# Mamba's x projection on the two column halves of the TensorE array, each with half of the tokens

## The chip, the cores and the metric

The kernel runs on one core of one Trainium2 chip. Its time is the device time of one launch in microseconds, taken as the median of three runs. The five engines of the core are named as in the profile: PE (TensorE, with its weight loads as PEld), DVE (VectorE), ACT (ScalarE), POOL (GpSimd) and SP (SyncE, which here issues the DMAs). Each works through its own instructions in order and waits on semaphores for the others.

## The reference

The program is a network of two blocks on an input of 4 images, 128 channels and 64 x 64 positions. Block 0 is a deformable neighbourhood attention followed by a recurrence over the 4096 positions; block 1 is a stack of eight Mamba layers followed by a mixture of experts. The change lies in the Mamba layers alone:

```python
def _mamba_layer(x, Wi, cw, cb, Wx, Wdt, bdt, Alog, Dp, Wo):
    xz = x @ Wi
    xi, z = jnp.split(xz, 2, axis=-1)                  # 256 channels each
    ...
    xc = jax.nn.silu(xc)                               # causal convolution of 4 taps before it
    dbl = xc @ Wx                                      # 256 -> 8 + 16 + 16
    dt_r = dbl[..., :DT_RANK]
    Bs = dbl[..., DT_RANK:DT_RANK + D_STATE]
    Cs = dbl[..., DT_RANK + D_STATE:]
    dt = jax.nn.softplus(dt_r @ Wdt + bdt)             # 8 -> 256
    dA = jnp.exp(dt[..., None] * A)
    dBx = (dt * xc)[..., None] * Bs[:, :, None, :]
    _, h = jax.lax.associative_scan(comb, (dA, dBx), axis=1)
    y = jnp.einsum('blds,bls->bld', h, Cs) + Dp * xc
    y = y * jax.nn.silu(z)
    return y @ Wo
```

"The x projection" is `xc @ Wx`: 256 channels in, 40 numbers out for each token.

## The kernel before

**Bodies.** The Mamba part works in bodies. A body is one layer of one image for 512 consecutive tokens (`TL`), and there are 8 chunks x 8 layers x 4 images = 256 of them. Channels lie on the 128 partitions, in two halves `h` (`NH` = 2). Everything is float32; a float32 matmul stands in the trace as two records of one call, a transpose as one.

**Slots.** A body has 16 slots `j`, one for each pair of states of one channel half. Per slot, PE makes the inputs of a scan (`inputs`, L1042, 8 calls with 64 rows each, or for one pair of states ACT writes the decay there instead), ACT makes the decays (`exps`, L1020), DVE runs two scans (`scan`, L1075), POOL multiplies by C every second slot (`times_c`, L1100), and PE adds the products up by transposing them into one bank (`add_up`, L1104). The inputs for slot j + 1 are issued in slot j, into one of two PSUM buffers; the adding up lags four slots behind.

**The rest of a body** (projections, convolution, gate, output projection, norm) is laid into the slots by a list written by hand, `PLAN`, one row a slot. `o` is the body that scans, `n` the next one, `q` the one before. Each row has a part ahead of the adding up and a part behind it. The rows that matter here are those of slots 7 to 13:

```
q.po1 n.edges o.by1 q.square q.pm | n.pz0 q.rstd
n.pz1 n.silu_z0 n.silu n.silu_z1 n.pd0 n.pd1 n.keep s.rr |
n.bt q.ru s.first n.spread n.B n.skip0 |
| q.u n.diag q.end
n.pt0 n.softplus0 n.pt1 n.dtx0 | o.leave0 n.softplus1
o.back0 o.x3 | z.fetch
| n.C0
```

(The first is slot 7; the fifth is slot 11, and slot 12 follows.) So `pd` (the x projection, `xproj`, L933) and `keep` (L939) belong to slot 8, B's transposes `bt` (`turn_b`, L994) and `spread` (L1003, L1009) to slot 9, the step's projection `pt` (`step_proj`, L967) and `softplus` (L973) to slot 11. In the profile a piece of a slot stands behind the scan inputs that are issued in the same slot.

**The recurrence of block 0** runs inside the same bodies: one of its steps is a small matmul (L683) and a tanh on ACT (L691), some 16 a body. Its last step is at 12,811 us; about 34 bodies follow without it.

**The layout before.** The projection's weights stand in the columns 0 to 39 of a 128-column block, with the 8 columns for dt a second time in the columns 64 to 71. `xproj` makes two calls, one per channel half, over all 512 tokens. `keep` copies all 128 rows of the result to SBUF (`dbl`, 512 columns), reordered in blocks of 64 tokens, and sends B and C to memory (`c_d`). `turn_b` transposes four blocks of 128 columns. `spread` takes 14 of the B columns and sends them by two DMAs onto the diagonals of a matrix in memory (`spare`), from which `diag` (L1014) fetches the moving operand of L1042. `step_proj` makes one call per channel half over all tokens, with the rows 0 to 63 for half 0 and 64 to 127 for half 1.

**Banks.** The pieces outside the scans share two PSUM banks, f0 and f1 (`BANK`): `pd` is in f1, `bt` in f0, `pt0` in f1, `pt1` in f0, and `back0` (L1132), the transpose back of the finished half of `o` in slot 12, in f0.

**SP** issues for each body two DMAs to `c_d`, two to `spare`, one `Bb`, one `diag` and four `Cb`, in that order (and others now and then).

Of the kernel before, what the change touches and what calls it, by code (L numbers as in the profile page):

```python
# [8 lines left out]
F32 = mybir.dt.float32  # L9
BF16 = mybir.dt.bfloat16  # L10
AF = mybir.ActivationFunctionType
# [9 lines left out]
P = 128  # L21
# [20 lines left out]
NH = 2  # L42
DI = NH * P
NS = 16
RK = 8
# [658 lines left out]
W_I, W_Z, W_X, W_DT = 0, DI, 2 * DI, 2 * DI + NH * P  # L704
# [42 lines left out]
def mamba(tc, ops, I, rec, x2_d, x3_d):  # L747
# [8 lines left out]
    nc = tc.nc  # L756
    NSLOT = NS // 2 * NH
    NB = TL // P
    HQ = TL // 2
    SP = NS // 2  # L760
    SP_B = SP - 1
    ND = 2 * SP_B
    AHEAD, LAG, HOLD = 3, 4, 2
    with ExitStack() as ctx:
# [4 lines left out]
        w = ctx.enter_context(tc.tile_pool(name="mwk", bufs=2))  # L769
# [3 lines left out]
        w1 = ctx.enter_context(tc.tile_pool(name="mw1", bufs=1))  # L773
# [7 lines left out]
        bdt = c.tile([P, DEPTH, NH], F32, name="bdt")  # L781
# [30 lines left out]
        def bank(what):  # L812

            name = f"f{BANK[what]}"
            return psf.tile([P, TL], F32, tag=name, name=name)
# [6 lines left out]
        def blocks(ap):  # L822

            return ap.rearrange("p (q b t) -> p b q t", q=2, b=NB)
# [103 lines left out]
        def xproj(o, h):  # L928

            if h == 0:  # L930
                o.pd = bank("pd")
            at = W_X + h * P
            nc.tensor.matmul(  # L933
                o.pd, o.given[:, at : at + P], o.xc[:, h, :], start=h == 0, stop=h == NH - 1
            )

        def keep(o):
            o.dbl = w1.tile([P, NB, 2, 64], F32, tag="dbl", name="dbl")
            nc.scalar.copy(o.dbl, blocks(o.pd))  # L939
            o.c_d = dr.tile([2 * NS, TL], F32, tag="c_d", name="c_d")  # L940
            for q in range(2):
                nc.sync.dma_start(
                    out=o.c_d[:, q * HQ : (q + 1) * HQ].rearrange("s (n t) -> s n t", n=NB),
                    in_=o.dbl[RK : RK + 2 * NS, :, q, :],
                )

        def give_b(o):
# [11 lines left out]
            )  # L959

        def step_proj(o, h):
            if h == 0:
                o.pt = {}
            o.pt[h] = bank(f"pt{h}")
            at = W_DT + h * P
            rows = slice(h * 64, (h + 1) * 64)
            nc.tensor.matmul(  # L967
                blocks(o.pt[h]), o.given[rows, at : at + P], o.dbl[rows], start=True, stop=True
            )

        def softplus(o, h):
            o.dt[h] = w3.tile([P, TL], F32, tag="dt", name="dt")
            nc.scalar.activation(o.dt[h], o.pt[h], AF.Softplus, bias=bdt[:, o.l, h : h + 1])  # L973

        def step_x(o, h):
            if h == 0:
# [13 lines left out]

        def turn_b(o):
            o.BT = bank("bt")
            for n in range(NB):
                nc.tensor.transpose(  # L994
                    o.BT[:, n * P : (n + 1) * P],
                    o.dbl[:, n].rearrange("p q t -> p (q t)"),
                    ops.ident,
                )

        def spread(o):  # L1000

            small = w.tile([P, NB, ND], F32, tag="bts", name="bts")
            nc.scalar.copy(small, o.BT.rearrange("p (n r) -> p n r", n=NB)[:, :, RK : RK + ND])  # L1003
            o.spare = spares[bodies.index(o) % len(spares)]
            for q in range(2):
                half = o.spare[q * 64 : (q + 1) * 64]
                line = half.ap[0][0]
                to = bass.AP(half.tensor, half.offset, [[line + ND, 64], [64 * ND, NB], [1, ND]])
                nc.sync.dma_start(out=to, in_=small[q * 64 : (q + 1) * 64])  # L1009

        def diag(o):

# [160 lines left out]
        def get(i):  # L1173
            return bodies[i] if 0 <= i < len(bodies) else None

        def table(name):
            return lambda o: nc.scalar.preload_act_table_set(name)

        halves = {
            "v": proj, "pz": proj_z, "silu_z": silu_z, "skip": skip_x, "pd": xproj, "pt": step_proj,  # L1180
            "softplus": softplus, "dtx": step_x, "turn": turn, "leave": leave, "back": turn_back,
            "gate": times_gate, "po": out_proj,
        }
# [7 lines left out]
            "fetch": fetch, "mean": mean, "var": lambda o: sums(o, o.x2, "var"),  # L1191
            "rv": lambda o: inverse(o, 1e-6), "rr": lambda o: rows(o, "rr"),
            "first": first_u, "silu": silu_x, "keep": keep, "spread": spread, "diag": diag,
            "B": give_b,
            "bt": turn_b, "square": square, "pm": lambda o: sums(o, o.sq, "pm"),
            "rstd": lambda o: inverse(o, 1e-5), "ru": lambda o: rows(o, "ru"), "u": norm,
            "x3": lambda o: fetch_x(o) if o.l == DEPTH - 1 else None,
# [23 lines left out]
        t = PRE  # L1221
        for i in range(-2, len(bodies) + 1):
            o, n, q = get(i), get(i + 1), get(i - 1)
            who = {"o": o, "n": n, "q": q, "m": get(i + 2), "a": o or q}
            s, z = get(i + 3), get(i + 4)
# [384 lines left out]
def attention_masks():  # L1610


    import numpy as np

    def seen(first, count, window, size):
        start = min(max(first - K // 2, 0), size - window)
        q = np.arange(first, first + count)
        k = np.arange(start, start + window)
        lo = np.clip(q - K // 2, 0, size - K)[:, None]
        return (k[None] >= lo) & (k[None] < lo + K)  # L1620

    r = [seen(f, ROWS, KR, H) for f in (0, ROWS, H - ROWS)]
    c = [seen(f, TC, KC, W) for f in (0, TC, W - TC)]
    m = np.stack([np.einsum("ak,bl->abkl", x, y).reshape(P, NKEY) for x in r for y in c], axis=1)
    return np.where(m, np.float32(0), np.float32(-1e30)).astype(np.float32)


def layouts(a):

    import numpy as np  # L1630

    def halves(v):
        return np.moveaxis(v.reshape(DEPTH, NH, P, *v.shape[2:]), 2, 0)

    f = {k: np.asarray(v) for k, v in a.items()}
    o = {}
    o["x"] = f["x"].reshape(B, P, L).transpose(1, 0, 2)
    o["proj"] = np.stack(
        [f[n].T for n in ("L0_conv_Wq", "L0_conv_Wk", "L0_conv_Wv", "L0_conv_Wo", "L0_ffn_W")],
        axis=1,  # L1640
    )
    o["V"] = f["L0_ffn_V"].T
    vec = [f[f"L0_conv_b{n}"] for n in "qkvo"]
    vec += [np.tile(f[f"L0_conv_{n}"], G) for n in ("off_dw_b", "ln_w", "ln_b")]
    vec += [f["L0_conv_rpe_b"], f["L0_ffn_gamma"], f["L0_ffn_beta"], np.tile(f["L1_ffn_gate_b"], 2)]
    o["vec"] = np.stack(vec, axis=1)
    o["dw"] = np.tile(f["L0_conv_off_dw_w"].reshape(HD, K * K), (G, 1))
    o["rpe"] = f["L0_conv_rpe_w"].reshape(P, 9)
    offw = np.zeros((P, 2, P), np.float32)
    for g in range(G):  # L1650
        ch = slice(g * HD, (g + 1) * HD)
        offw[ch, :, ch] = f["L0_conv_off_pw_w"].T[:, :, None]
    o["offw"] = offw
    o["mask"] = attention_masks()
    w_in = f["L1_conv_W_in"]
    o["m_taps"] = halves(f["L1_conv_conv_w"])
    given = np.zeros((DEPTH, P, W_GIVEN), np.float32)
    given[:, :, W_I : W_I + DI] = w_in[:, :, :DI]
    given[:, :, W_Z : W_Z + DI] = w_in[:, :, DI:]
    for h in range(NH):  # L1660
        ch = slice(h * P, (h + 1) * P)
        given[:, :, W_X + h * P : W_X + h * P + RK + 2 * NS] = f["L1_conv_W_xproj"][:, ch]
        given[:, :, W_X + h * P + 64 : W_X + h * P + 64 + RK] = f["L1_conv_W_xproj"][:, ch, :RK]
        given[:, :, W_OUT + h * P : W_OUT + (h + 1) * P] = f["L1_conv_W_out"][:, ch]
        given[:, h * 64 : h * 64 + RK, W_DT + h * P : W_DT + (h + 1) * P] = f["L1_conv_W_dt"][:, :, ch]
    o["m_given"] = given
    o["m_cb"] = halves(f["L1_conv_conv_b"])
    o["m_bdt"] = halves(f["L1_conv_b_dt"])
    o["m_skip"] = halves(f["L1_conv_D_skip"])
    o["m_A"] = halves(f["L1_conv_A_log"])  # L1670
    o["m_rms"] = f["L1_conv_rms_w"].T
    o["gate"] = f["L1_ffn_gate_w"].T

    w1, w2 = f["L1_ffn_weight1"], f["L1_ffn_weight2"]
    t = w1[:, :P].reshape(2, 4, 4, 2, P, HID).transpose(0, 2, 4, 3, 1, 5)
    o["w1"] = t.reshape(8, P, 8 * HID)
    t = w2[:, :HID].reshape(2, 4, 4, 2, NHC, P, P).transpose(0, 2, 5, 3, 1, 4, 6)
    o["w2"] = t.reshape(8, P, 8 * HID)
    o["b1"] = np.repeat(w1[:, P].reshape(2, P // B, HID), B, axis=1)
    o["b2"] = w2[:, HID].T  # L1680
    return {k: np.ascontiguousarray(v) for k, v in o.items()}
# [16 lines left out]
```

## Time and profile before

| | us |
|---|---|
| median of 3 runs | 14,895.22 (14,884.57 to 14,900.8) |
| the profiled execution | 14,892.08 |
| its span, first to last instruction | 14,890.3 |
| busy DVE, POOL, ACT (share of the span) | 12,974.0 (87%), 12,589.8 (85%), 10,980.2 (74%) |
| x projection, L933: 1,024 records of 128x512 | mean 592 ns |
| pt, L967: 1,024 records of 64x512 | mean 589 ns |
| B's transposes, L994: 1,024 records of 128x128 | mean 287 ns |
| keep, L939: 256 copies of 128x512 | mean 586 ns |
| softplus, L973: 512 of 128x512 | mean 690 ns |
| granted TensorE clock over the span | 0.984 |

A record of PE starts before the one ahead of it has ended, so its duration is a latency; what a record costs is the time from its start to the start of the next. Durations of the other engines overlap by about 0.1 us in the same way.

The Mamba part reaches from about 1,924 us to 14,608 us. The first scans of successive bodies stand 48.6 us apart in most bodies while the recurrence runs, and 49.4 us in every fourth, which also turns a new block of the recurrence's input. After the recurrence they stand 48.3 to 51.4 us apart, 49.8 in the mean.

### The profile page before, as it was taken

The page shows a single profiled execution, that of the slowest core. Times are in us where ns is not written, and L with a number is a line of the kernel's source. Part 1 is how long each engine was busy: PE and PEld are TensorE (multiplying, and loading weights), DVE is VectorE, ACT ScalarE, POOL GpSimd, SP SyncE. Part 2 cuts the span into 40 slices and gives each one's busy share as a digit, 9 for nine tenths or more (in the row PEclk, how much of TensorE's full clock was granted, in tenths as well). Part 3 has the DMA queues.
Part 4 walks back from the last instruction along what each step waited for, and adds up shares of the span by engine and source line. Part 5 has one row for each costly group of instructions (what it writes and reads, how often), then busy time and mean ns, then how long its engine had stood idle before and what let it go on. Part 6 is the DMA issues. An engine that isn't in the chain of part 4 may idle for free. (4 is left out here: it accounts for less than half of the span.)

```text
span 14890.3 us, 307789 instructions
## 1 busy us (share of the span) xinstructions
PE 14160.7 (95%) x124378; PEld 10821.2 (73%) x124378; DVE 12974.0 (87%) x16043; ACT 10980.2 (74%) x21400; POOL 12589.8 (85%) x5760
## 2 busy tenths in 40 slices
PE   7999989999999999999999999999999999999996
PEld 3444467777777777777777777777777777777775
DVE  8997079998999899999998999989999999989994
ACT  6887267777777777777777777777777777777773
POOL 5564079999999999999999999999999999999993
PEclk8999999999999999999999999999999999999998
DMA  0000034434443434343444344344434343434344
GB/s 23 26 26 23 29 122 144 144 136 148 142 147 135 152 137 150 132 151 138 149 142 144 137 149 142 138 145 145 146 136 151 138 149 133 154 131 145 133 146 184
DMA packets 600044, 1914.56 MB, mean 129 GB/s; under 512 B 347488, under 2 KB 347872, under 8 KB 434272
## 3 DMA queue, kind: packets, MB, share of 16 engines
q1 hardware_dynamic: 598480, 1894.60, 36.1%
q8 instruction: 984, 16.12, 0.4%
q14 instruction: 436, 3.57, 0.1%
q10 hardware_dynamic: 144, 0.26, 0.0%
HBM read 1823.10 MB, written 71.57 MB: 127 GB/s over the span
## 5 line engine op out<-in xcount | busy, mean ns | idle before, releaser
L1100 POOL TENSOR_TENSOR hs<-hs,Cb 128x2048 f32<-128x2048 f32 x2048 | 9300.9, 4543 | 749.0 <-DVE state L1092 562.3
L1075 DVE TENSOR_TENSOR_SCAN hs<-dA,state,dBx 128x512 f32<-128x512 f32 x7168 | 8808.2, 1267 | 700.2 <-PE dBx L1042 561.3
L1020 ACT ACTIVATE dA<-dt,A 128x512 f32<-128x512 f32 x7168 | 4730.4, 716 | 11.6 <-DVE hs L1075 5.5
L1104 PE MATMUL yT<-ident,hs 128*128 128x128 f32 x32768 | 4376.9, 277 | 30.4 <-POOL hs L1100 30.2
L1042 PE MATMUL dBx<-diag,dtxT 64*128 64x128 f32 x57344 | 4195.3, 283 | 27.1 <-DVE hs L1075 20.1
L1104 PEld LDWEIGHTS yT<-ident,hs 128*128 128x128 f32 x32768 | 3785.4, 147 | 433.6 <-issue 349.2
L1042 PEld LDWEIGHTS dBx<-diag,dtxT 64*128 64x128 f32 x57344 | 3509.4, 187 | 800.7 <-issue 741.3
L683 PEld LDWEIGHTS p<-z,vt 128*128 128x128 f32 x8192 | 1283.9, 189 | 881.8 <-ACT z L691 401.8
L691 ACT ACTIVATE z<-p 128x4 f32<-128x4 f32 x4096 | 702.3, 171 | 1396.6 <-PE p L683 1368.8
L683 PE MATMUL p<-z,vt 128*128 128x4 f32 x8192 | 1453.7, 248 | 107.1 <-ACT z L691 98.4
L1075 DVE TENSOR_TENSOR_SCAN hs<-dAp,state,hs 128x512 f32<-128x512 f32 x1024 | 1273.3, 1273 | 296.7 <-POOL hs L1063 296.7
L1063 POOL TENSOR_TENSOR hs<-Bb,dtx 128x512 f32<-128x512 f32 x1024 | 1284.9, 1280 | 0.0
L904 DVE SCALAR_TENSOR_TENSOR xc<-f,taps,xc 128x511 f32<-128x511 f32 (+2 forms) x1536 | 1115.8, 726 | 53.4 <-ACT z L691 49.3
L1020 ACT ACTIVATE dAp<-dt,A 128x512 f32<-128x512 f32 x1024 | 708.8, 692 | 491.6 <-DVE hs L1075 470.1
L279 DVE SCALAR_TENSOR_TENSOR acc<-qp,dww,acc 128x512 f32<-128x512 f32 x1184 | 892.4, 754 | 25.6
L979 POOL TENSOR_TENSOR dtx<-dt,xc 128x512 f32<-128x512 f32 x512 | 651.6, 1273 | 217.5 <-ACT dt L973 217.5
L293 POOL TENSOR_TENSOR off<-off,to 128x512 f32<-128x512 f32 x288 | 366.4, 1272 | 412.7 <-ACT to L291 400.0
L1020 ACT ACT_TABLE_LOAD x511 | 655.6, 1283 | 9.0
L898 ACT ACTIVATE xc<-f,taps 128x512 f32<-128x512 f32 x512 | 350.7, 685 | 414.7 <-PE f L895 281.1
L919 PE MATMUL f<-u,given 128*128 128x512 f32 x1024 | 600.6, 670 | 3.8 <-DVE xc L904 3.8
L847 PEld LDWEIGHTS f<-avg,sq 128*128 128x128 f32 x2048 | 257.0, 197 | 466.0 <-ACT sq L1148 466.0
L895 PE MATMUL f<-u,given 128*128 128x512 f32 x1024 | 567.0, 636 | 0.8 <-DVE u L868 0.8
(235 smaller groups left out, 15160.8 us busy)
## 6 DMA issues: line engine op xcount, KB each, us to landing
Cb<-c_d SPq DMA_DIRECT2D x1024, 1024.0 KB, 7.2
diag<-spare SPq DMA_DIRECT2D x256, 1792.0 KB, 8.8
Bb<-c_d SPq DMA_DIRECT2D x256, 512.0 KB, 4.8
given<-in_m_given_dram SPq DMA_DIRECT2D x64, 640.0 KB, 8.6
slab<-in_w_dram SPq DMA_DIRECT2D x60, 512.0 KB, 9.9
x<-x_d SPq DMA_DIRECT2D x96, 256.0 KB, 3.0
c_d<-dbl SPq DMA_DIRECT2D x512, 32.0 KB, 1.6
x_d<-x SPq DMA_DIRECT2D x63, 256.0 KB, 3.2
```

Source lines behind the costliest of these rows:

```text
L279: nc.vector.scalar_tensor_tensor(rows(to), x, dww[:, t : t + 1], rows(o.acc), ALU.mult, ALU.add)
L683: nc.tensor.matmul(self.p[:, k, :], self.vt, self.before, start=False, stop=True, skip_group_check=True)
L691: nc.scalar.activation(self.z[:, k, :], self.p[:, k, :], AF.Tanh, scale=0.5)
L904: nc.vector.scalar_tensor_tensor(x, o.v[h][:, : TL - k], taps[:, o.l, h, DC - 1 - k : DC - k], x, ALU.mult, ALU.add)
L919: nc.tensor.matmul(o.pz[h], o.given[:, at : at + P], o.u, start=True, stop=True)
L979: nc.gpsimd.tensor_tensor(to, blocks(o.dt[h]), blocks(o.xc[:, h, :]), ALU.mult)
L1020: nc.scalar.activation(o.dA[j][:, k, :], o.dt[h], AF.Exp, scale=A[:, o.l, h, n : n + 1])
L1042: nc.tensor.matmul(o.dBx[j][:, at : at + 64, :], o.dtxT[h][row, n, :], o.diag[row, n, :, 2 * sp : 2 * sp + 2], start=True, stop=True,)
L1063: nc.gpsimd.tensor_tensor(hs[:, k, :].rearrange("p (q n t) -> p q n t", n=NB, q=2), o.Bb[:, k, :].rearrange("p (q n t) -> p q n t", n=NB, ...
L1075: nc.vector.tensor_tensor_scan(hs[:, k, :], o.dA[j][:, k, :], hs[:, k, :] if sp == SP_B else o.dBx[j][:, :, k], state[:, o.l, o.b, h, s : ...
L1100: nc.gpsimd.tensor_tensor(hs, hs, o.Cb[f], ALU.mult)
L1104: nc.tensor.matmul(o.yT[:, n, :], x[:, n * P : (n + 1) * P], ops.ident, start=start and n == 0, stop=True, is_transpose=True, skip_group_c ...
```

## The change

The x projection is split by tokens. Its weights now stand twice, whole, in the columns 0 to 39 and 64 to 103. For each channel half there are two calls of 64 columns and 256 tokens: the first half of the tokens goes to the PSUM partitions 0 to 63, the second half to 64 to 127. So the result is 256 columns wide, `keep` copies 256 columns, and only two blocks are transposed. `step_proj` makes its four calls at the place of `pt0`: each takes the 64 rows that hold its tokens, one bank per token half, both channel halves beside each other in it. `softplus` needs two instructions per channel half, one from each bank. `spread` sends four DMAs of half the size instead of two.

```diff
             if h == 0:
                 o.pd = bank("pd")
-            at = W_X + h * P
-            nc.tensor.matmul(
-                o.pd, o.given[:, at : at + P], o.xc[:, h, :], start=h == 0, stop=h == NH - 1
-            )
+            for q in range(2):
+                at = W_X + h * P + q * 64
+                nc.tensor.matmul(
+                    o.pd[q * 64 : (q + 1) * 64, 0:HQ], o.given[:, at : at + 64],
+                    o.xc[:, h, q * HQ : (q + 1) * HQ], start=h == 0, stop=h == NH - 1,
+                )
 
         def keep(o):
-            o.dbl = w1.tile([P, NB, 2, 64], F32, tag="dbl", name="dbl")
-            nc.scalar.copy(o.dbl, blocks(o.pd))
+            o.dbl = w1.tile([P, HQ], F32, tag="dbl", name="dbl")
+            nc.scalar.copy(o.dbl, o.pd[:, 0:HQ])
             o.c_d = dr.tile([2 * NS, TL], F32, tag="c_d", name="c_d")
             for q in range(2):
                 nc.sync.dma_start(
-                    out=o.c_d[:, q * HQ : (q + 1) * HQ].rearrange("s (n t) -> s n t", n=NB),
-                    in_=o.dbl[RK : RK + 2 * NS, :, q, :],
+                    out=o.c_d[:, q * HQ : (q + 1) * HQ],
+                    in_=o.dbl[q * 64 + RK : q * 64 + RK + 2 * NS, :],
                 )
...
         def step_proj(o, h):
-            if h == 0:
-                o.pt = {}
-            o.pt[h] = bank(f"pt{h}")
-            at = W_DT + h * P
-            rows = slice(h * 64, (h + 1) * 64)
-            nc.tensor.matmul(
-                blocks(o.pt[h]), o.given[rows, at : at + P], o.dbl[rows], start=True, stop=True
-            )
+            if h:
+                return
+            o.pt = [bank(f"pt{q}") for q in range(2)]
+            for h in range(NH):
+                at = W_DT + h * P
+                for q in range(2):
+                    rows = slice(q * 64, (q + 1) * 64)
+                    nc.tensor.matmul(
+                        o.pt[q][:, h * HQ : (h + 1) * HQ], o.given[rows, at : at + P], o.dbl[rows],
+                        start=h == 0, stop=True, skip_group_check=True,
+                    )
 
         def softplus(o, h):
             o.dt[h] = w3.tile([P, TL], F32, tag="dt", name="dt")
-            nc.scalar.activation(o.dt[h], o.pt[h], AF.Softplus, bias=bdt[:, o.l, h : h + 1])
+            for q in range(2):
+                nc.scalar.activation(
+                    o.dt[h][:, q * HQ : (q + 1) * HQ], o.pt[q][:, h * HQ : (h + 1) * HQ], AF.Softplus,
+                    bias=bdt[:, o.l, h : h + 1],
+                )
...
         def turn_b(o):
             o.BT = bank("bt")
-            for n in range(NB):
-                nc.tensor.transpose(
-                    o.BT[:, n * P : (n + 1) * P],
-                    o.dbl[:, n].rearrange("p q t -> p (q t)"),
-                    ops.ident,
-                )
+            for m in range(NB // 2):
+                here = slice(m * P, (m + 1) * P)
+                nc.tensor.transpose(o.BT[:, here], o.dbl[:, here], ops.ident)
 
         def spread(o):
-            small = w.tile([P, NB, ND], F32, tag="bts", name="bts")
-            nc.scalar.copy(small, o.BT.rearrange("p (n r) -> p n r", n=NB)[:, :, RK : RK + ND])
+            small = w.tile([P, NB // 2, 2, ND], F32, tag="bts", name="bts")
+            turned = o.BT[:, 0 : NB // 2 * P].rearrange("p (m q r) -> p m q r", m=NB // 2, q=2)
+            nc.scalar.copy(small, turned[:, :, :, RK : RK + ND])
             o.spare = spares[bodies.index(o) % len(spares)]
-            for q in range(2):
-                half = o.spare[q * 64 : (q + 1) * 64]
-                line = half.ap[0][0]
-                to = bass.AP(half.tensor, half.offset, [[line + ND, 64], [64 * ND, NB], [1, ND]])
-                nc.sync.dma_start(out=to, in_=small[q * 64 : (q + 1) * 64])
+            line = o.spare.ap[0][0]
+            for b in range(2):
+                for q in range(2):
+                    half = o.spare[q * 64 : (q + 1) * 64, b]
+                    to = bass.AP(half.tensor, half.offset, [[line + ND, 64], [2 * 64 * ND, NB // 2], [1, ND]])
+                    nc.sync.dma_start(out=to, in_=small[b * 64 : (b + 1) * 64, :, q])
```

The host's layout of the weights follows: `W_xproj` whole in both halves of the columns, and `W_dt` of both channel halves on the rows 0 to 7 and on the rows 64 to 71. The size of what is loaded stays.

## The prediction

> **What bounds the kernel now.** I read the busy line first, then the waits, then stretches of the timeline.
>
> ```profile
> PE 14160.7 (95%) x124378; PEld 10821.2 (73%) x124378; DVE 12974.0 (87%) x16043; ACT 10980.2 (74%) x21400; POOL 12589.8 (85%) x5760
> ```
>
> No engine is idle for long, so the order decides. Windows of the Mamba part, with and without the recurrence (columns: length; busy us of PE, PEld, DVE, ACT, POOL; granted clock; DMA share; GB/s):
>
> ```profile
> 4000.00:6000.00 2000.00, 1952.76 (x18120) 1573.04 (x18118) 1837.47 (x2080) 1539.77 (x2936) 1850.68 (x756) 1.00 0.41 144
> 13100.00:14300.00 1200.00, 1105.40 (x9944) 864.54 (x9942) 1088.96 (x1230) 864.75 (x1354) 1085.43 (x433) 0.97 0.39 138
> ```
>
> With the recurrence PE is busy 98% of the time. The waits say what is left, and who waits for PE:
>
> ```profile
> DVE hs L1075 <- PE dBx L1042: 561.3, 559, 21.1
> ...
> PE f L847 <- ACT sq L1148: 254.2, 256, 2.4
> ```
>
> The numbers are the total in us, how many times, and the longest; the Mamba part has 256 bodies. PE has one wait of weight, 1.0 us a body for the square in slot 7. DVE waits for PE 2.2 us a body. So in the 222 bodies with the recurrence **PE's queue sets the period**, and what leaves it counts in full until another engine is late.
>
> PE around the projection in one such body (start, length, records):
>
> ```profile
> 8042.85 1.12 PE L919 MATMUL f<-u,given 128*128 128x512 f32 x2
> 8043.81 1.88 PE L933 MATMUL f<-xc,given 128*128 128x512 f32 x4
> 8045.52 1.04 PE L1104 MATMUL yT<-ident,hs 128*128 128x128 f32 x8
> 8046.49 1.16 PE L1042 MATMUL dBx<-diag,dtxT 64*128 64x128 f32 x16
> 8047.59 0.66 PE L994 MATMUL f<-ident,dbl 128*128 128x128 f32 x4
> 8048.08 0.60 PE L862 MATMUL f<-ident,r 128*128 128x128 f32 x4
> 8048.52 1.04 PE L1104 MATMUL yT<-ident,hs 128*128 128x128 f32 x8
> ```
>
> Read the starts: the projection holds PE for 8045.52 - 8043.81 = 1.71 us, 0.43 a record of 512 columns, 0.21 for 256; a transpose costs 0.11 (four in 0.44). After dBx the DVE scan of slot 10 starts at 8047.70, having waited 1.03 us.
>
> **The x projection, -0.57 us a body.** Four calls of 64 columns are eight records of 256. If the two column halves stream together they take 4 x 0.213 = 0.85 us. That they do is shown by the attention's product, whose four column groups have different moving operands:
>
> ```profile
> 830.82 1.02 PE L306 MATMUL po<-on,offw 128*128 128x512 f32 x2
> 831.77 0.86 PE L433 MATMUL pa<-at,vk 110*32 110x128 f32 x24
> 832.56 0.33 PE L441 MATMUL pa<-ident,rx 128*128 128x128 f32 x1
> 832.72 0.27 PE L411 MATMUL pt<-ident,exps 128*110 128x128 f32 x1
> ```
>
> 24 records of 128 columns in 832.56 - 831.77 = 0.79 us is six groups of four. Six transposes' worth of streaming would be 0.65, so the array's other shape costs something: 831.77 - 830.82 = 0.95 against 0.86 for two records is 0.09 going in, the first group takes some 0.02 more, 0.11 is left for coming out, and the next record's 0.16 instead of 0.11 is 0.05: together 0.27-0.29. [...] By the row the projection is 0.85 + 0.29 = 1.14, by the rule 1.18. I take the row: 1.71 - 1.14 = **-0.57**. Ends: -0.4, and +0.3 if the halves do not overlap.
>
> **B's transposes, -0.22.** Two of 0.11 go. Those left are the same operation on the same shape.
>
> **keep and spread, nothing.** The copy has 256 columns instead of 512. 586 ns at 512 and 182 at 56 columns (the copy of L1003) give 0.89 ns a column, so it is 0.23 us shorter. It is off PE's path: two streams of PE, 2.07 us, lie between its start and bt. The copy of L1003 keeps its 56 columns.
>
> **SP, nothing.** c_d's two DMAs stay. spare's go from two of 0.62 us issue to four of half the pieces: 0.32 each by the row of Cb (128 pieces), 0.62 at worst, so the last is issued 0 to 1.25 us later, and Bb and diag behind it. Behind these stand the four Cb, which wait for POOL in any case (3,422 us in total). diag lands 8.8 us after its issue and is first used 11.2 us after it in the median, so 2.4 us cover it (1.5 in the worst twentieth). SP itself has waited 24 us a body for keep by then. If the cover went, PE would stall in slot 15 by the difference.
>
> **The step's projection, 0.** Before: two row halves side by side, 2 x 0.43 and the change of shape, 8052.82 to 8053.77. After: four pairs of 0.21, no further change of shape. All four calls now come before the first softplus, which is PE's order already. Bank f0 is free then: its reader, the copy of L1003, ended 4 us earlier. f1 is held until the second softplus instead of the first; its next user is turn0 in slot 14.
>
> **softplus, +0.14.** This is what is late next:
>
> ```profile
> 8053.77 1.09 PE L1104 MATMUL yT<-ident,hs 128*128 128x128 f32 x8
> 8053.87 0.69 ACT L973 ACTIVATE dt<-f,bdt 128x512 f32<-128x512 f32 x1 [0.18 <-PE f L967]
> ...
> 8054.90 0.58 ACT L1126 COPY yTs<-yT 128x512 f32<-128x512 f32 x1 [0.34 <-PE yT L1104]
> 8055.38 0.69 ACT L973 ACTIVATE dt<-f,bdt 128x512 f32<-128x512 f32 x1
> ...
> 8056.13 0.66 PE L1132 MATMUL f<-ident,yTs 128*128 128x128 f32 x4
> ```
>
> At 0.89 ns a column a softplus of 256 lasts 0.46 us, and two follow each other at 0.59 - 0.23 = 0.36, so a pair takes 0.83 instead of 0.69. The first pair is covered by the 0.34 us that ACT waits for yT. The second is not: it ends at 8056.07, and PE's transpose back, which needs its bank, starts at 8056.13. So PE stalls by about 0.14 (0.09 if the instructions overlap more, 0.2 if less). Behind the stalled instruction stand the transposes of xD, yT and the inputs of slot 14, for which DVE waits 0.81 us already. POOL's dtx comes 0.1 later at most, in a wait of 0.93 us that shrinks with PE.
>
> **Sum.** -0.57 - 0.22 + 0.14 = -0.65 us a body. Does the rest follow? DVE at slot 10 waits 1.03 and gets its inputs 0.57 earlier. It then works without a gap to slot 13, where it waits 0.45 for PE, then 0.81 in slot 14; PE is 0.79 and 0.65 earlier there. POOL waits for DVE or ACT 3.3 us a body at places that move along. The square of slot 7 depends on PE's own output projection. 222 x 0.65 = 144 us. In the last 34 bodies the same slot 10 wait (1.03) stands on DVE's path but the transposes don't, and ACT's longer softplus does: 0.57 - 0.17 = 0.4, 14 us. 14,892 - 158 = 14,734 for the profiled execution; the median stands 3 us above it: I predict **14,735 us**.
>
> **Rivals.**
> 1. *Another loop takes over: 14,815.* Without the recurrence, with some 5 us less for PE, undisturbed bodies still take 48.32. If that is a floor of DVE, POOL and ACT, then three bodies in four gain 48.58 - 48.32 = 0.26 and the fourth 0.65: 0.36 x 222 = 80. For it: those 48.32. Against: that loop also runs through the projection, since its slot 10 waits the same 1.03. Chance 0.17.
> 2. *The clock, slower: 15,040.* The clock fell to half for single stretches of 3.4 or 6.8 us, beginning 22 to 26 us into a body, just behind the square's wait: in ten bodies or so with the recurrence, but in more than half of those after it, where that wait is 2.0 us. Half-clocked bodies take up to 51.4 instead of 48.3, 3 us. [...] By the row nothing happens (the wait of slot 7 keeps its length and the projection comes 4 us after it: 14,735). If the wait grows, for instance because DVE falls behind PE, 55% of the bodies could pay 2.4 us: 1.3 - 0.65 = +0.65 x 222 = 147. It decides from 22% of the bodies at 3 us each. Chance 0.11.
> 3. *The halves do not overlap: 14,950.* 8 x 0.213 + 0.29 instead of 1.71, less 0.22, plus 0.14: +0.21 x 256 = 54. Against it stand L433's rows. Chance 0.04.
> 4. *No change,* the gain being eaten by a stall behind softplus or diag. Chance 0.05.
>
> **How the numbers follow.** The forecast has 0.63, with its own range 14,695 to 14,775 (softplus' and the projection's ends, a few half-clocked bodies more or fewer). The range given reaches to the first rival, for 0.80 together: its upper end, 14,860, allows that rival a further 45 us (0.2 us a body, the difference of the bounds of softplus and the projection), its lower end takes the projection's and softplus' better bounds. Changes under 0.2%, 30 us, cannot be told from none. Faster: 0.63 + 0.17 = 0.80; same 0.05; slower 0.11 + 0.04 = 0.15.
>
> **What would show it.** Right: the projection's eight records within 1.15 us; DVE's wait in slot 10 near 0.45; bodies 47.9 us apart; PE waiting some 0.14 us for the second softplus. Wrong: pace of 0.21 for single records there, a granted clock under 0.98 before 12,800 us, PE waits for DVE at L1042, or bodies stuck at 48.3.

## The result and the profile after

The changed kernel takes 14,734.65 us (median of 4 runs, 14,726.2 to 14,745.7); the kernel before, on the same chip, 14,893.86 (4 runs, 14,884.57 to 14,900.8). The ratio is 0.9894, with a 95% interval of 0.9879 to 0.991. The forecast was 14,735. The profiled execution took 14,727.09 us with a span of 14,725.3; that is 165 us less than the profiled execution of before, where 158 were forecast.

The busy line of the page after:

```profile
PE 13977.1 (95%) x125914; PEld 10770.0 (73%) x125914; DVE 12960.7 (88%) x16043; ACT 11003.0 (75%) x21912; POOL 12593.5 (86%) x5760
```

PE has 1,536 records more (four more per body for the projection, four more for the step's projection, two fewer transposes: 6 x 256) and is busy 184 us less. Its share is 95% as before, since the span shrank with it. This is how a gain on the engine that bounds looks: shares hardly move. The same windows as before (length; busy us of PE, PEld, DVE, ACT, POOL; granted clock; DMA share; GB/s):

```profile
4000.00:6000.00 2000.00, 1949.26 (x18541) 1584.00 (x18542) 1857.98 (x2105) 1559.62 (x3053) 1873.53 (x767) 1.00 0.40 145
13100.00:14300.00 1200.00, 1101.48 (x10252) 872.15 (x10253) 1102.81 (x1247) 882.47 (x1424) 1103.97 (x441) 0.97 0.39 140
```

DVE and POOL do 20 and 23 us more in the same 2,000 us, 1.1 and 1.2%; the bodies became 1.3% shorter. The waits that count, from the list of waits after (total us, times, longest):

```profile
DVE hs L1084 <- PE dBx L1051: 503.0, 772, 21.3
...
POOL hs L1109 <- DVE state L1101: 392.2, 534, 19.2
...
PE f L847 <- ACT sq L1157: 253.4, 256, 2.4
```

PE's wait for the square stayed (254.2 before). DVE waits 58 us less for PE; POOL's wait for DVE was 562.3 and is 392.2. The first scans of successive bodies now stand 47.97 us apart in the median while the recurrence runs (48.59 before). Added up, the bodies 0 to 217 take 133 us less (10,770 to 10,637), the 37 bodies behind them, 218 to 254, take 34 less (1,845 to 1,811); the end of the last body cannot be read in this way. These 37 are called the last bodies below; the recurrence still runs in the first two of them.

Now the place of the change, in the timeline after (start, length, engine, line, records):

```profile
7826.94 1.08 PE L934 MATMUL f<-xc,given 128*64 128x256 f32 x8
7827.96 1.09 PE L1113 MATMUL yT<-ident,hs 128*128 128x128 f32 x8
...
7830.07 0.44 PE L1005 MATMUL f<-ident,dbl 128*128 128x128 f32 x2
...
7830.19 1.28 DVE L1084 TENSOR_TENSOR_SCAN hs<-dA,state,dBx 128x512 f32<-128x512 f32 x1 [0.47 <-PE dBx L1051]
...
7830.35 0.60 PE L862 MATMUL f<-ident,r 128*128 128x128 f32 x4
```

Read the starts again. The projection holds PE for 7827.96 - 7826.94 = 1.02 us where it held it for 1.71. The transposes hold it for 0.28 where it was 0.49. The scan of slot 10 waits 0.47 us instead of 1.03 (the number in brackets is the idle time before the instruction, with what ended it). The records of the projection start in pairs 5 to 7 ns apart, and the pairs 0.21 to 0.27 apart: the two halves stream together.

The place where something was to be given back, the softplus:

```profile
7836.15 0.84 ACT L980 ACTIVATE dt<-f,bdt 128x256 f32<-128x256 f32 x2 [0.19 <-PE f L972]
...
7837.65 0.84 ACT L980 ACTIVATE dt<-f,bdt 128x256 f32<-128x256 f32 x2
...
7838.16 0.39 PE L683 MATMUL p<-z,vt 128*128 128x4 f32 x2
...
7838.55 0.66 PE L1141 MATMUL f<-ident,yTs 128*128 128x128 f32 x4
```

The second pair ends at 7838.49 and `back0` starts 0.06 us behind it, at 7838.55. From the last record of L683 ahead of it to `back0` there are now 0.26 us in the median, 0.11 before: PE stalls 0.15 us longer.

And SP, in the same timeline (the four issues for `spare` together), with its row in the timeline of before:

```profile
7831.21 2.53 SPq L1018 DMA_DIRECT2D spare<-bts  x4
```

```profile
8049.07 1.25 SPq L1009 DMA_DIRECT2D spare<-bts  x2
```

So an issue costs about 0.6 us whether it carries 256 pieces, as before, or 128. `diag` is issued 10.6 us ahead of its first use in the median (11.2 before) and lands after 9.1 (8.8 before).

### The profile page after: what moved, and what is told of

The parts are those of the page before. It is cut to its first block, busy times and chain, and to the rows that moved or that the text cites. A ratio compares the mean times of both kernels' runs of the same rounds, so it can differ in the third digit from the quotient of the medians.

```text
span 14725.3 us, 311884 instructions
## 1 busy us (share of the span) xinstructions
PE 13977.1 (95%) x125914; PEld 10770.0 (73%) x125914; DVE 12960.7 (88%) x16043; ACT 11003.0 (75%) x21912; POOL 12593.5 (86%) x5760
## 5 line engine op out<-in xcount | busy, mean ns | idle before, releaser
L1109 POOL TENSOR_TENSOR hs<-hs,Cb 128x2048 f32<-128x2048 f32 x2048 | 9303.2, 4544 | 594.0 <-DVE state L1101 392.2
L683 PEld LDWEIGHTS p<-z,vt 128*128 128x128 f32 x8192 | 1284.3, 189 | 882.8 <-ACT z L691 402.3
L683 PE MATMUL p<-z,vt 128*128 128x4 f32 x8192 | 1453.9, 248 | 108.8 <-ACT z L691 100.1
```

The costliest lines, as they stand in the source:

```text
L683: nc.tensor.matmul(self.p[:, k, :], self.vt, self.before, start=False, stop=True, skip_group_check=True)
L1109: nc.gpsimd.tensor_tensor(hs, hs, o.Cb[f], ALU.mult)
```

## The experiments

The theory: PE's queue sets the period everywhere, so each part counts in full (projection, transposes, softplus), and SP's longer issue is covered. The rivals left: parts that do not add up because another loop is near, or time that the clock gives and takes. In what follows, "half-clock stretches" are the stretches of the granted-clock records in which it was 0.5; before the change they add up to 96 us in the bodies 0 to 217 and 116 us in the last bodies, after it to 96 and 89. "Bodies N us apart" is from here on the median of the bodies up to 217 that have no half clock in them or in the body before: it shows the pace without the clock. Sums of bodies and half clock come from the one traced execution of each kernel. Executions of one kernel lie up to 32 us apart (the changed kernel's 20), so a difference of ten or so between such sums says little. The kernel before was run again beside each batch of experiments (medians of 14,891.87 to 14,898.85 us), the changed kernel was not. The expectations stand as they were written before each run.

**The softplus in two pieces, nothing else.** On the kernel before:

```diff
-            nc.scalar.activation(o.dt[h], o.pt[h], AF.Softplus, bias=bdt[:, o.l, h : h + 1])
+            for q in range(2):
+                part = slice(q * HQ, (q + 1) * HQ)
+                nc.scalar.activation(
+                    o.dt[h][:, part], o.pt[h][:, part], AF.Softplus, bias=bdt[:, o.l, h : h + 1]
+                )
```

> The kernel before with nothing changed but softplus in two instructions of 256 columns per channel half. Theory (PE's queue sets the period and the second softplus ends last before the transpose back): PE stalls 0.15 us a body there, 222 x 0.15 = 33 us slower than before, 14,927 us, with bodies 48.7 us apart. Rival (another loop at 48.3 us sets the period, or ACT has room there): under 5 us of difference, bodies at 48.58.

14,936.34 us (7 runs), ratio to before 1.003 (1.0019 to 1.0041); bodies 48.73 us apart, +0.14. 44 us slower: 0.14 x 256 = 36, and some more in the last bodies. So two softpluses of 256 columns where there was one of 512 cost what the forecast said, and PE pays it: from the last record of L683 to `back0` there are 0.26 us in the median here too.

**The second softplus ahead of the adding up.** The remedy, on the changed kernel: the `PLAN` row of slot 11 lets ACT run all four pieces before it copies `yT`.

```diff
-n.pt0 n.softplus0 n.pt1 n.dtx0 | o.leave0 n.softplus1
+n.pt0 n.softplus0 n.pt1 n.softplus1 n.dtx0 | o.leave0
```

> The changed kernel with the second softplus ahead of the copy of yT (leave0) on ACT, same instructions otherwise. Theory: the stall of 0.15 us ahead of the transpose back goes, since the copy that then ends last ends some 0.1 us before PE gets there; 222 x 0.15 = 33 us faster than the changed kernel, 14,702 us, bodies 47.8 us apart. Rival (48.3, now 47.95, is a floor of the other engines): no difference, 14,735.

14,720.02 us (4 runs), ratio 0.9884 (0.9871 to 0.9898); 18 us above the expectation. Its timeline:

```profile
7821.21 1.57 ACT L980 ACTIVATE dt<-f,bdt 128x256 f32<-128x256 f32 x4 [0.19 <-PE f L972]
7822.65 0.60 ACT L1135 COPY yTs<-yT 128x512 f32<-128x512 f32 x1
...
7823.23 0.39 PE L683 MATMUL p<-z,vt 128*128 128x4 f32 x2
7823.47 0.64 PE L1141 MATMUL f<-ident,yTs 128*128 128x128 f32 x4
```

`back0` follows 0.24 us behind the start of the group of L683, where it was 7838.55 - 7838.16 = 0.39: the stall is gone (in the median the step from the last record of L683 to `back0` is 0.11 again), and the bodies are 47.85 us apart (-0.12; three bodies in four went from 47.96 to 47.80). But added up the bodies 0 to 217 took only 17 us less (10,637 to 10,620), with 109 us of half clock instead of 96, and the last bodies became 15 us longer, 1,826 instead of 1,811, with 140 us of half clock instead of 89. The mechanism held; more than half of its gain went where the half clock grew. Hence the runs on the clock below.

**Four transposes again.** The changed kernel turns its two blocks twice, into all four quarters of the bank:

```diff
-            for m in range(NB // 2):
-                here = slice(m * P, (m + 1) * P)
-                nc.tensor.transpose(o.BT[:, here], o.dbl[:, here], ops.ident)
+            for m in range(NB):
+                here = slice(m % 2 * P, (m % 2 + 1) * P)
+                nc.tensor.transpose(o.BT[:, m * P : (m + 1) * P], o.dbl[:, here], ops.ident)
```

> The changed kernel with B's two transposes issued twice, into columns that nothing reads. Theory: 0.22 us a body back on PE's queue, 222 x 0.22 = 48 us slower than the changed kernel, 14,783 us, bodies 48.17 apart. Rival (PE has room after the projection, the transposes' saving was hidden): 14,735, bodies at 47.95.

14,816.32 us (5 runs), ratio 0.9947 (0.9935 to 0.996): 33 us above the expectation. Bodies 48.19 us apart, +0.22 as expected, 48 us for 218 of them. The last bodies took 22 us more than in the changed kernel, 0.58 each. Only two of them, behind the recurrence, are undisturbed (no half clock in the body or the one before); they are 47.93 and 47.94 us apart instead of 47.71, +0.23. With 9 us due by that, the rest of the 22 goes with the clock (113 us of half clock instead of 89). The traced execution, 14,799.98, is the shortest of the five; the others lie 12 to 17 us above it.

**No tiling.** The projection by calls of 128 columns over half the tokens, with as much streaming as the two halves side by side but no other shape of the array. It leaves out the projection of the second half of the tokens:

```diff
-            for q in range(2):
-                at = W_X + h * P + q * 64
-                nc.tensor.matmul(
-                    o.pd[q * 64 : (q + 1) * 64, 0:HQ], o.given[:, at : at + 64],
-                    o.xc[:, h, q * HQ : (q + 1) * HQ], start=h == 0, stop=h == NH - 1,
-                )
+            at = W_X + h * P
+            nc.tensor.matmul(
+                o.pd[:, 0:HQ], o.given[:, at : at + P], o.xc[:, h, 0:HQ],
+                start=h == 0, stop=h == NH - 1,
+            )
```

> The changed kernel with the x projection as two calls of 128 columns over the first 256 tokens, in the array's whole shape; the projection of the other 256 tokens is left out (their rows hold the first half's values). The same four streams of 256 columns pass, without the change of shape. Theory (changing the shape costs 0.31 us a body: 0.09 in, 0.16 around the groups and out, 0.06 at the next record): 222 x 0.31 = 69 us faster than the changed kernel, 14,666 us. [...] Rival (the shape is free, or its price is hidden): 14,735.

14,677.76 us (4 runs), ratio 0.9858 (0.9844 to 0.9871), 12 us above the expectation; bodies 47.67, -0.30. The last bodies took 14 us more than in the changed kernel, with 137 us of half clock instead of 89. Two neighbouring rows of its timeline:

```profile
7831.75 1.03 PE L933 MATMUL f<-xc,given 128*128 128x256 f32 x4
7832.61 1.04 PE L1112 MATMUL yT<-ident,hs 128*128 128x128 f32 x8
```

7832.61 - 7831.75 = 0.86 us for four records of 256, against 1.02 for the four pairs; the rest of the 0.30 lies ahead of the first record (0.43 us instead of 0.52 from the record before it) and behind the next (0.11 instead of 0.165). So the other shape of the array cost 0.30 us a visit here, in and out together. The forecast had 0.27 to 0.29 from the attention's rows.

**The calls in another order.** In the change the two column halves alternate (half 0, half 1, half 0, half 1). If it is the neighbourhood of the calls that makes pairs, an order by token half should break them:

```diff
+            if h == 0:
+                return
             for q in range(2):
-                at = W_X + h * P + q * 64
-                ...
+                for h in range(NH):
+                    at = W_X + h * P + q * 64
+                    ...
```

> The changed kernel with the x projection's four calls in another order: both channel halves of the first tokens, then both of the second, so that neighbours in PE's queue mostly belong to the same column half. Theory (column halves stream together only where neighbouring calls are on different halves): only the boundary overlaps, 7 or 6 streams of 0.213 instead of 4, +0.43 to +0.64 us a body, 222 x that = 95 to 142 us slower, 14,830 to 14,877 us. Rival (the array finds the other half's calls further back in the queue): 14,735.

14,722.81 us (4 runs), ratio 0.9887 (0.9873 to 0.99), bodies 47.98. My theory fell, its rival held:

```profile
7824.73 1.09 PE L937 MATMUL f<-xc,given 128*64 128x256 f32 x8
7825.76 1.09 PE L1116 MATMUL yT<-ident,hs 128*128 128x128 f32 x8
```

The whole row of L937 holds PE for 7825.76 - 7824.73 = 1.03 us, against 1.02. Two calls of one half follow each other, four records, and yet the records start in pairs 13 ns apart (7 ns in the changed kernel), at the pace of 0.21 us. So the third call was taken ahead of the second. The trace bears this out. The wait for the second channel half's `xc` belongs to the second call, whose first weight load would be the third of the eight in the order of the program; in 255 of 256 bodies it stands on the fifth. The one exception is body 1, where the second call had to wait for that `xc`:

```profile
1975.97 0.19 PEld L937 LDWEIGHTS f<-xc,given 128*64 128x64 f32 x2 [1.00 <-ACT xc L911]
1976.58 0.63 PEld L937 LDWEIGHTS f<-xc,given 128*64 128x64 f32 x6 [0.42 <-ACT xc L911]
```

There it stands on the third: the first call ran alone, and nothing passed the waiting one. So the calls do come to PE in the order of the program. In the other 255 bodies the third call, for the free half, passed the second, which is for the same half as the first; in this one body it did not pass one that waited for its input. Why it passes, no run here shows.

**SP's issues, twice.** First each `spare` DMA was issued twice:

```diff
-                    nc.sync.dma_start(out=to, in_=small[b * 64 : (b + 1) * 64, :, q])
+                    for _ in range(2):
+                        nc.sync.dma_start(out=to, in_=small[b * 64 : (b + 1) * 64, :, q])
```

> The changed kernel with each of the four spare DMAs issued twice (the same bytes to the same place). SP's row says 0.605 us an issue whatever the size, so the last one is issued 2.4 us later, and diag behind it. diag is issued 10.6 us before its first use and lands after 9.1, so 1.5 us are covered. Theory: PE stalls about 0.9 us a body for diag in slot 15: 222 x 0.9 = 200 us slower than the changed kernel, 14,935 us (14,880 to 14,990). Rival (SP's place in the order doesn't matter): 14,735.

16,969.92 us (4 runs), ratio 1.1397 (1.1379 to 1.1414). A bad experiment: it changes two things. The second write to a place waits for the first to land, so it is not four issues that were added but four issues and four landings. SP's row in the timeline:

```profile
8032.40 11.58 SPq L1019 DMA_DIRECT2D spare<-bts  x8
```

and a line of SP's own waits, then one of PE's:

```profile
SPq L1019 <- DMA spare<-bts: 1404.2, 1024, 3.2
```

```profile
PE dBx L1052 <- DMA diag<-spare: 1726.6, 256, 15.3
```

SP takes 11.58 us instead of 2.53, 1,404.2 / 256 = 5.5 of them waiting for first writes, and PE waits for `diag` in every body, 1,726.6 / 256 = 6.7 us. The clock went down with it: in the bodies 0 to 217 the half clock is 1,839 us instead of 96, most of it beginning within that wait, and the granted clock of the span is 0.926. It shows where the cover ends, not the price of an issue. The second form sends four more DMAs to places of their own, behind `spare`'s:

```diff
+            for q in range(4):
+                aside = dr.tile([64, NB // 2, ND], F32, tag=f"aside{q}", name="aside")
+                half = small[q // 2 * 64 : (q // 2 + 1) * 64, :, q % 2]
+                nc.sync.dma_start(out=aside, in_=half)
```

> The changed kernel with four more small DMAs of the same size behind spare's four, each to a place of its own in memory that nothing reads. At 0.605 us an issue Bb and diag are issued 2.4 us later. diag is issued 10.6 us before its first use in the changed kernel and lands after 9.1. Theory: PE waits 0.9 us a body for diag, 222 x 0.9 = 200 us slower than the changed kernel, 14,935 us, more if the wait lets the clock drop. Rival (the cover is longer than the medians say, or diag lands sooner when it starts later): under 30 us, 14,735 to 14,765.

15,154.39 us (4 runs), ratio 1.0173 (1.0157 to 1.0188): missed by 220 us. Four issues for `aside` take 2.55 us in its timeline: an issue costs 0.6 here too. A line of its waits:

```profile
PE dBx L1055 <- DMA diag<-spare: 248.2, 180, 9.8
```

In the changed kernel PE waited for `diag` 8 times, 11.9 us in all; here 180 times. The cover of 1.5 us is used up and PE stalls in slot 15, where the step from the record ahead of the inputs to their first grows by 1.2 us a body (0.9 expected; the list of waits puts some of these down to other names). But the bodies grow by 1.6 in the mean of all up to 217. Some 0.2 of it may be half clock (181 us in the first 218 bodies instead of 96; half of these 85 us more, spread over the bodies, is 0.2); about 0.2 I cannot account for. What it settles: the added 1.25 us of issue in the change stay under the cover, by 1.5 us, and a further 2.5 would not.

**PE's wait for the square.** The last open stall of PE, 1.0 us a body, stands in slot 7. At its end or up to 3 us behind it, 22 to 26 us into a body, begin all half-clock stretches of the last bodies and 24 of the 96 us in the first 218. The other 72 stand at another place, 8 to 11 us into the first and every 32nd body; in every 32nd PE has then waited 5 to 6 us for a `z` of the recurrence (L683). Two ways to deal with it were tried. First the sums `pm` that wait for the square were moved behind the adding up, so that PE has work meanwhile:

```diff
-q.po1 n.edges o.by1 q.square q.pm | n.pz0 q.rstd
+q.po1 n.edges o.by1 q.square | q.pm n.pz0 q.rstd
```

> The changed kernel with the sums of squares (pm, L847) moved behind the adding up of slot 7, so that eight transposes fill PE's wait for the square. Theory of the clock (short stretches of half clock come from the square's wait together with the sums' tiny matmuls): the half-clock stretches of the last 34 bodies go for the most part, 34 x 1.2 = 41 us, and some 15 us of those before; the period itself stays at 47.8 to 47.97, since the wait only moves to the x projection, which needs ACT's silu at the same time as now. 14,650 to 14,690 us. Rival 1 (the stretches depend on total idleness, which stays): 14,735. Rival 2 (PE's wait of 0.85 us is simply gained): 14,735 - 222 x 0.85 = 14,545.

14,779.18 us (5 runs), ratio 0.9926 (0.9914 to 0.9938): 90 us above the expectation and 45 above the changed kernel. Its waits:

```profile
PE f L919 <- DVE r L855: 198.4, 254, 1.1
...
PE f L847 <- ACT sq L1157: 52.9, 36, 1.5
```

The wait for the square fell from 253.4 to 52.9 us, and a new one of 198.4 stands at the next piece: `pz0` uses the bank of `pm`, and now DVE must first have read the sums (`r`). The bodies stayed at 47.98. The wait was moved, not removed, and the half clock of the first 218 bodies rose from 96 to 171 us: seven stretches behind the wait became 29. The theory of the clock in the expectation, that these would go, fell as well.

> The two moves of order together, the second softplus ahead of the copy of yT and the sums behind the adding up. If they add: 0.14 x 222 = 31 us below the run with the sums moved, 14,620 to 14,660 us. If the clock eats what the first saves, as it did in the last bodies when it was alone (15 us saved of 33): 14,640 to 14,675.

Both moves (this one and that of the softplus): 14,763.78 us (4 runs), ratio 0.9914 (0.99 to 0.9927), about 100 us above the expectation; 208 us of half clock in the first 218 bodies, 181 in the last ones.

Then the wait was filled: three bf16 matmuls of zeros (512 columns each), written into the bank that `pm` then overwrites. The helper for it, `busy`, is one that the kernel uses elsewhere.

```diff
             o.ms = bank(what)
+            if what == "pm":
+                for _ in range(3):
+                    rec.busy(o.ms, NB)
```

> The changed kernel with three bfloat16 matmuls of zeros (512 columns each, some 0.21 us) on PE ahead of the sums of squares, where PE waits 0.85 us for the square in any case; their result is overwritten by the sums. The period of a body stays at 47.97. Theory of the clock (a half-clock stretch follows a window of 3.4 us in which PE streamed too little): the stretches (14 before the last 34 bodies, 17 in them) go for the most part: some 25 us in the first and up to 1.2 x 34 = 41 us in the last, 14,670 to 14,700 us. Rival (matmuls of zeros do not count, or the wait is not what lets it drop): 14,735. Other rival (they do not fit in the wait): slower, bodies above 48.0.

14,690.78 us (4 runs), ratio 0.9863 (0.9847 to 0.988), as expected: 44 us faster than the changed kernel with more work on PE (its slowest run, 14,697.52, is faster than the changed kernel's fastest, 14,726.2). PE's timeline at slot 7:

```profile
7814.28 0.81 PE L655 MATMUL f<-still 128*128 128x512 bf16 x3
7815.20 1.05 PE L850 MATMUL f<-avg,sq 128*128 128x1 f32 x8
```

and its window over the last bodies:

```profile
12900.00:14100.00 1200.00, 1117.08 (x10549) 876.94 (x10546) 1127.45 (x1276) 899.55 (x1452) 1131.13 (x452) 1.00 0.40 144
```

The granted clock of that window is 1.00; a window of the same length in the last bodies of the changed kernel, 13,100 to 14,300, has 0.97. The half-clock stretches of the last bodies went from 89 us to 20, and these bodies from 48.96 us to 48.15 in the mean (1,811 to 1,782 in sum). The typical body with the recurrence did not change (47.99), nor did the undisturbed ones among the last (47.72). In the first 218 bodies the 24 us of half clock behind the wait for the square are gone to the last stretch; the 65 us that remain all stand 9 to 11 us into the first and every 32nd body, at the place that was not filled. So what was gained is clock, 29 of the 41 us between the two traced executions in the last bodies. For the expectation's theory of the clock: in the traces before and after, the half-clock stretches begin and end on one grid of 3.4 us steps, and of the 31 in the bodies 0 to 254 of the changed kernel 30 begin right behind a step in which PE was busy under 75% (1.33 of 3.41 us ahead of the one at 13,242.1, 2.52 ahead of the one at 2,650.5). But 40 other steps at full clock were as idle, and no half clock followed them.

**Filling and softplus together**

> Both: the three matmuls of zeros in the wait, and the second softplus ahead of the copy of yT. If the softplus move is worth 0.14 us a body once the clock stays up: 33 us below the run with the filled wait alone, 14,640 to 14,665 us. If the clock drops all the same: 14,720, as the softplus move alone.

14,674.74 us (4 runs), ratio 0.9852 (0.9837 to 0.9867): 10 us above the expectation, 60 faster than the changed kernel, and the fastest of all. It is the two edits above at once. Bodies 47.83; in the first 218 there is again no half clock behind the wait for the square. But the last ones lost part of what the filling had gained (68 us of half clock, 1,793 us in sum).

## Why the prediction was right

**The total: right for the most part for its reasons, in part by errors that cancel.** Forecast 158 us off the profiled execution, measured 165. The bodies with the recurrence gave less than forecast (133 us for 218 of them, where 0.65 x 218 = 142 were due), the last ones more (34 instead of 14). That the median came out at the forecast to the microsecond is luck.

**The projection, -0.57: measured -0.55.** From the start of the record ahead of it to the first record behind it 2.145 us became 1.537 (-0.61), and that record's own pace went from 0.11 to 0.165 (+0.06). The change of the array's shape cost 0.31 in the timeline (0.09 going in, 0.16 in the pairs and coming out, 0.06 behind) and 0.30 by the run without it; the forecast from L433 was 0.27 to 0.29. No run shows the rule by which the forecast also has 1.18 for the whole projection; in its place the runs show 1.71 - 0.55 = 1.16.

**The transposes, -0.22: confirmed** by the timeline and by putting them back (+0.22 a body).

**The softplus, +0.14: confirmed** three ways: 0.15 of stall in the trace, +0.14 when it is split alone, and the stall gone when it is moved off PE's path (-0.12 in the median body, -0.16 in three of four).

**SP: "0.32 each by the row of Cb" was wrong,** "0.62 at worst" was right: 0.605 an issue in the median (0.616 before), with half of the pieces. The conclusion stood because the bound had been carried to the cover: 1.25 us later, of 2.4. The cover shrank to 1.5, partly since `diag` also comes 0.6 us nearer to its use as PE speeds up.

**Sum, -0.65: measured -0.62** in every kind of body: 48.59 to 47.97 in most, 49.43 to 48.82 in every fourth.

**Last bodies, "0.57 - 0.17 = 0.4, 14 us": the term that was mis-sized.** They gave 34. Two things were wrong. The forecast took DVE's path to set the period there, so that the transposes would not count. But the undisturbed bodies went from 48.32 to 47.71, the full -0.61; putting the transposes back adds 0.23, moving the softplus off takes 0.31 away (47.40, in the run that also fills the wait). Each edit of PE's queue counts there too, although PE is busy only 92% of the time. The waits of 24 of these bodies in the changed kernel show what its idle time is:

```profile
PE f L847 <- ACT sq L1157: 57.4, 24, 2.4
PE yT L1113 <- POOL hs L1109: 20.6, 24, 1.1
```

That is 2.4 us a body for the square and 0.9 for POOL. Both were as long before (57.6 and 20.4), and PE is idle for about 4.0 us of an undisturbed body before the change as after it. So these waits did not give way when PE's queue became shorter, they moved with it. The gain of it is 0.61 x 37 = 23 us. The other 11 of the 34 go with the clock, 89 us at half clock instead of 116; the forecast's sum had nothing for them, so they are luck.

**Rival 1, a floor at 48.32:** fell with the same rows. It was no floor of other engines, but the pace of PE.

**Rival 2, the clock:** did not decide, as the wait of slot 7 kept its length and the half clock of the first 218 bodies stayed at 96 us (most of which stands at every 32nd body, a place that the forecast did not name). But what half clock can cost was under-priced: in the last bodies it was some 26 us when the softplus was moved (15 more where 0.31 x 37 = 11 less was due) and some 13 when the transposes came back (22 where 9 was due), and filling the wait was worth 44 us, more than any scheduling move tried. The "few half-clocked bodies more or fewer" of the forecast are 10 to 30 us, as much as a whole step of its sum.

**Rivals 3 and 4** fell: the records stand in pairs, and nothing behind softplus or `diag` ate the gain beyond the 0.15 us of stall.

## What to carry over

Where one engine's queue sets the period, cost each edit by the starts of that engine's records, and take even a stage with 8% of idle time as bound by it until you know what the idle time waits for. Carry the worst bound of a hidden cost to the end of its cover: here the price of the DMA issue was wrong by a factor of two and nothing followed, but 2.5 us more on that queue cost 420 us. And where half clock begins behind a wait on PE, moving the wait may not help: moved to another place it cost 45 us, filled with idle matmuls it gave 44. Look for the other waits of that kind too: the one at every 32nd body is still unfilled, with 65 us of half clock behind it.

## What the hardware showed that I had not expected

- The two column halves streamed together in either order of the calls: 1.03 us for the four pairs with the calls of one half next to each other, 1.02 with the halves alternating. In the first order the third call starts ahead of the second (the wait for the second channel half stands on the fifth weight load instead of the third, in 255 of 256 bodies).
- A DMA issue on SP cost 0.6 us for 256 pieces as for 128, on a diagonal as into the plain blocks of `aside`. Eight that write each place twice took 11.58 us, 5.5 of them waiting for the first writes to land. The issues of `Cb`, 0.32 us, and of `diag`, 0.34, are cheaper; why, no run here settles.
- Matmuls of zeros kept the clock up: three of them a body, 0.8 us in all, took the half clock of the last bodies from 89 us to 20, and that behind the same wait in the first 218 from 24 us to none. The stretches are multiples of 3.4 us (the last one ends with the trace) that lie, in the traces before and after, on one grid of that step through the whole span. Waits for the square of 0.8 us (with the recurrence) and 2.4 us (without) stood ahead of them here; how little activity is too little no run here settles.
